# Graph attention, layer 3: the row of R of heads 1 to 3 by one bf16 matmul per block over an exact split in three parts

## The chip, the cores and the metric

The kernel runs on one core of one Trainium2 chip. The metric is the time of one execution on the device, in microseconds (us), lower is better. The engines are named as in the profile: PE (TensorE matmul), PEld (TensorE weight load), DVE (VectorE), ACT (ScalarE), POOL (GpSimd), SP (SyncE).

## The reference, cut to what matters

Sixteen graphs of 1024 nodes with 256 features pass four attention layers. In each layer the features are normalized, clipped at zero and projected, and every node takes a softmax-weighted mean over its neighbours. Layer 3 has four heads of 64 features each:

```python
h = einsum('bnd,hde->bhne', x, W)
e_src = einsum('bhne,hte->bhtn', h, a_src)
e_dst = einsum('bhne,hte->bhtn', h, a_dst)
weight = leaky_relu(e_src[:, :, 0, :, None] + e_dst[:, :, 0, None, :], 0.01)   # adj is 0 or 1: one type
attention = softmax(where(adj == 0, -1e9, weight), axis=-1)
dst = einsum('bhij,bhje->bhie', attention, h) + bias
out = relu(dst) + h          # then a layer norm over the 64 features of each head
```

The kernel doesn't form the logits. With s_i = e_src and d_j = e_dst, the exponential of leaky_relu(s_i + d_j) is the larger of exp(s_i + d_j) and exp(0.01 (s_i + d_j)). A factor exp(s_i) cancels in the softmax, and exp(0.01 d_j) is put into the values. What remains of a weight is max(C_j, R_i) where an edge is, and 0 elsewhere, with C_j = exp(0.99 d_j) and R_i = exp(-0.99 s_i). The change concerns how R gets to where it is used.

## The kernel before, in words

A short path (`short_path`) does the work; `general_path` is entered only if a flag says that the exponentials would be out of range. Each graph is a batch, worked by the generator `batch(b)`. Nodes are laid out as 8 blocks of 128: node blocks i are columns of a result, node blocks j are what is summed over and lie on the partitions.

For a layer, `weigh` makes the weights, transposed: 8 tiles of 128 nodes j by 1024 nodes i, in float32. It needs R_i as a row of 1024 elements that is the same on all 128 partitions. R is at hand as columns: for layer 3 in the tile `ex` (128 nodes x 8 blocks x 12 numbers: exp(0.01 d), C and R of the four heads). So `weigh` takes the PSUM tile `row` (two banks, one buffer for the whole kernel) and fills it by 8 transposes of PE (L314). Each has the column of one block, broadcast to 128 x 128, as its stationary operand and the identity as the moving one. Then DVE makes one weights tile per block j (L318), max(row, C_j) times the mask of edges. A list, `row_taken`, keeps two streams from holding the row at once.

In layers 0 to 2 (`attend`) PE multiplies the weights with the values V (L409, 128x128 tiles of the array). `project` turns the new features for the next layer (L290), ACT copies them (L292), PE projects them (L297), and ACT and DVE take them out of PSUM (L361, L365; in the projection for layer 3 L381, L382, with POOL writing V3 and adding beta, L384 to L389).

In layer 3 the loop over the heads h goes: the row and the weights of head 0 are started ahead of it; then for each head the row of head h + 1 is started, PE adds up the totals and values of head h in four 128x32 tiles of the array (L517), ACT copies the two accumulators (L579), PE turns them (L586, L594), and DVE, ACT and POOL scale and normalize (L487 to L502).

PSUM is full: `acc0` and `acc1` with two banks each, two buffers of `misc` (turned tiles of all kinds), and the row.

What sets the order: there are two streams, one of the even and one of the odd batches. Each generator yields estimated times, and the stream that is behind goes next (`streams`, with an offset `LAG`). So layer 3 of one batch is traced beside layers 0 to 2 of the next. The framework then lays each engine's queue at build time from this order and its own estimates of when inputs are ready; only instructions under `keep_in_program_order` are pinned. Each engine works its queue in order and waits on semaphores that the framework sets.

Of the kernel before, what the change touches and what calls it, by code (L numbers as in the profile page):

```python
# [32 lines left out]
F32 = mybir.dt.float32  # L33
BF = mybir.dt.bfloat16
# [7 lines left out]
P = 128  # L42
# [5 lines left out]
SLOPE = 0.2  # L48
L3_SLOPE = 0.01

REACH = 75.0


# [6 lines left out]
def short_path(ctx: ExitStack, tc: tile.TileContext, ins: dict, out: bass.AP, bad: bass.AP):  # L60

    nc = tc.nc
    x, adj = ins["x"], ins["adj"]
    B, N, D = x.shape
# [20 lines left out]
    make_identity(nc, ident)  # L85
    minus_half = const.tile([P, 1], F32, name="minus_half")
    nc.vector.memset(minus_half, -0.5)
    ones = const.tile([P, P], F32, name="ones")
    nc.vector.memset(ones, 1.0)

    squares = const.tile([P, B, NI], F32, name="squares")
    inverses = const.tile([P, B, NI], F32, name="inverses")
# [69 lines left out]
    def prepare():  # L162

        forms = [
            (SLOPE, 1 - SLOPE, SLOPE - 1),
            (-SLOPE, SLOPE - 1, 1 - SLOPE),
            (0.0, 1.0, -1.0),
            (L3_SLOPE, 1 - L3_SLOPE, L3_SLOPE - 1),  # L170
        ]
        scratch = [edges.tile([P, N], F32, name="weights1") for _ in EXT]

        def extend(l: int):
            n = EXT[l] // 3
            engine = nc.vector if l == 0 else nc.gpsimd
            for c, factor in enumerate(forms[l]):
                engine.tensor_scalar_mul(
                    W[l][:, :, D + c * n : D + (c + 1) * n],
                    wa[:, :, l : l + n, 0 if c == 2 else 1],  # L180
                    factor,
                )

        def fetch(l: int):
            def begin(dst: bass.AP, src: bass.AP):
                fetched = nc.sync.dma_start(dst, src)
                if l > 0:
                    tc.keep_in_program_order(fetched)

            if l < 3:  # L190
                begin(W[l][:, :, :D], ins[f"L{l}_W"].rearrange("(k p) o -> p k o", p=P))
                begin(scratch[l][:, : 2 * D], on_all_partitions(ins[f"L{l}_a"], 2 * D))
                return
            for k in range(NK):
                begin(
                    W[3][:, k, :D].rearrange("p (h e) -> p h e", h=H),
                    ins["L3_W"][:, ts(k, P), :].rearrange("h p e -> p h e"),
                )
            for s, name in enumerate(("L3_a_src", "L3_a_dst")):
                first = ins[name]  # L200
                begin(
                    scratch[3][:, ts(s, D)].rearrange("p (h e) -> p h e", h=H),
                    bass.AP(tensor=first.tensor, offset=first.offset, ap=[[0, P], [T * E, H], [1, E]]),
                )
            for t, a in ((bias, ins["L3_bias"]), (gamma, ins["L3_gamma"]), (beta, ins["L3_beta"])):
                begin(t, on_all_partitions(a, D))

        for l in range(3):
            fetch(l)
            yield  # L210
            for k in range(NK):
                for s in range(2):
                    prod = work.tile([P, D], F32, name="above", bufs=2)
                    made = nc.vector.tensor_tensor_reduce(
                        prod, W[l][:, k, :D], scratch[l][:, ts(s, D)], op0=ALU.mult, op1=ALU.add,
                        scale=1.0, scalar=0.0, accum_out=wa[:, k, l, s : s + 1],
                    )
                    if l > 0:
                        tc.keep_in_program_order(made)
            extend(l)  # L220
            yield
        fetch(3)
        yield
        for s in range(2):
            for k in range(NK):
                prod = work.tile([P, D], F32, name="above", bufs=2)
                tc.keep_in_program_order(
                    nc.vector.tensor_mul(prod, W[3][:, k, :D], scratch[3][:, ts(s, D)])
                )
                nc.vector.tensor_reduce(  # L230
                    wa[:, k, 3:, s], prod.rearrange("p (h e) -> p h e", h=H), AX.X, ALU.add
                )
        extend(3)

        tc.keep_in_program_order(nc.vector.tensor_scalar_add(beta, beta, -2.0))
        tc.keep_in_program_order(nc.vector.tensor_scalar_mul(gamma, gamma, ROOT_E))

        groups = (3 + H) * 2
        wa2 = small.tile([P, NK, groups], F32, name="wa2", bufs=1)
        nc.vector.tensor_mul(wa2, wa.rearrange("p k g s -> p k (g s)"), wa.rearrange("p k g s -> p k (g s)"))  # L240
        norms = psum.tile([P, 3 + H, 2], F32, name="misc")
        for k in range(NK):
            nc.tensor.matmul(
                norms.rearrange("p g s -> p (g s)"), ones, wa2[:, k],
                start=(k == 0), stop=(k == NK - 1),
            )
        both = small.tile([P, 3 + H], F32, name="both", bufs=1)
        nc.vector.tensor_reduce(both, norms, AX.X, ALU.add)
        worst = small.tile([P, 1], F32, name="worst", bufs=1)
        nc.vector.tensor_reduce(worst, both, AX.X, ALU.max)  # L250
        nc.vector.tensor_scalar(bad, worst, REACH * REACH / (2.0 * D), None, op0=ALU.is_gt)
        yield
# [50 lines left out]

    row_taken = []

    def weigh(b: int, column, c, op, into: list):


        while row_taken:
            yield 0.25  # L310
        row_taken.append(b)
        r = psum.tile([P, N], F32, name="row", bufs=1)
        for i in range(NI):
            nc.tensor.transpose(r[:, ts(i, P)], column(i).to_broadcast([P, P]), ident)  # L314
        yield 0.5
        for j in range(NI):
            w = edges.tile([P, N], F32, name=f"weights{b % 2}")
            nc.vector.scalar_tensor_tensor(w, r, c(j), masks[b][:, j // 2, :, j % 2], op0=op, op1=ALU.mult)  # L318
            into.append(w)
            if j == NI - 1:  # L320
                row_taken.pop()
            yield 0.5

    def start(behind, b: int):

        for t in behind:
            if row_taken == [b]:
                return
            yield t
# [19 lines left out]
    def batch(b: int):  # L349
# [43 lines left out]
        def attend(l: int, V: bass.AP, finish, then: int):  # L393

            weights = []
            behind = weigh(
                b, lambda i: V[:, i, D + 2 : D + 3], lambda j: V[:, j, D + 1 : D + 2],
                ALU.min if l == 1 else ALU.max, weights,
            )
            yield from start(behind, b)  # L400
            following = begin(then) if then < 3 else begin3()
            steps = iter(())
            accs = {}
            sums = small.tile([P, NI], F32, name="sums_of_x")

            def product(i: int, j: int):
                if j == 0:
                    accs[i] = accumulator(b)[:, : D + 1]
                nc.tensor.matmul(  # L409
                    accs[i], weights[j][:, ts(i, P)], V[:, j, : D + 1],  # L410
                    start=(j == 0), stop=(j == NI - 1),
                )


            for j in range(NI):
                next(behind)
                product(0, j)
                product(1, j)
                if b == 0 and j == NI - 1:


                    next(preparing)
                    if l == 0:
                        next(loading[1])
                    next(preparing, None)
                yield 0.9
            for _ in behind:
                pass
            for i in range(NI):
                if i > 1:  # L430
                    for j in range(NI):
                        product(i, j)
                acc = accs.pop(i)
                finish(i, acc, sums[:, i : i + 1])
                if i != 0:
                    yield 3.6
                if i % 2 == 1:

                    yield from steps
                    steps = project(b, then, xb, sums, i // 2, following[1])  # L440
                yield from islice(steps, 1)
            yield 1.0
            yield from steps
            return following[0]
# [61 lines left out]
        def weigh3(h: int):  # L506
            if h == H:
                return iter(())
            return weigh(
                b, lambda i: ex[:, i, 2 * H + h : 2 * H + h + 1],  # L510
                lambda j: ex[:, j, H + h : H + h + 1], ALU.max, weights,
            )

# [31 lines left out]

        behind = weigh3(0)
        yield from start(behind, b)
        for h in range(H):


# [461 lines left out]
```

## Time and profile before

| What | Value |
|---|---|
| Median of 3 runs | 3025.95 us (3025.94 to 3026.56) |
| Profiled execution | 3025.06 us, span 3023.3 us, granted PE clock 0.993 |
| Busy time: PE, PEld | 2905.2 us (96% of the span), 1960.1 us (65%) |
| Busy time: DVE, ACT, POOL | 2112.7 us (70%), 1092.1 us (36%), 964.5 us (32%) |
| Chain that ended last | PE 78%, DVE 12%, POOL 4%, ACT 4%, issue 2% |
| Rows of R of layer 3 (L314) | 512 PE instructions, 68.9 us busy, 276 ns each |
| Weights of layer 3 (L318) | 512 DVE instructions, 631.2 us busy, 1276 ns each |

Busy time is the time in which at least one instruction of the engine runs. PE's instructions overlap, so the busy time of a group is less than its count times its mean; the distance between two starts is what an instruction costs. The chain is followed back from the last instruction: at each step to what released it, or to the instruction before it on its engine.

### The profile page before, as it was taken

How to read it: one execution, taken by the hardware profiler on the slowest of the kernel's cores; microseconds unless marked ns; L12 is line 12 of the kernel's file. 1: busy time of each engine (PE TensorE's matmuls, PEld its weight loads, DVE VectorE, ACT ScalarE, POOL GpSimd, SP SyncE). 2: the span in 40 equal slices, each digit the busy share in tenths (PEclk: the TensorE clock that was granted, in tenths of full speed). 3: DMA queues.
4: the chain of work that ended last, by engine and by line, in shares of the span. 5: the costliest groups of instructions: out<-in, count | busy, mean ns of one | idle time of the engine just before them, and what ended most of it. 6: DMA issues, size and time to landing. Idle time of an engine off the chain costs nothing.

```text
span 3023.3 us, 44588 instructions
## 1 busy us (share of the span) xinstructions
PE 2905.2 (96%) x16774; PEld 1960.1 (65%) x16774; DVE 2112.7 (70%) x4467; ACT 1092.1 (36%) x3009; POOL 964.5 (32%) x1455
## 2 busy tenths in 40 slices
PE   7999999999999999999999999999999999999985
PEld 5775857658576675756758566585766857667551
DVE  5657687676866758677576875758667686675756
ACT  2333424243343433424334243433434334243331
POOL 2124324142232423324233242432324234242333
PEclk9999999999999999999999999999999999999997
DMA  7204023030321403122040220302204031110101
GB/s 122 37 8 63 29 29 56 8 49 29 36 49 14 71 2 49 36 28 57 5 50 31 29 56 8 50 29 32 53 11 56 19 50 36 15 29 5 19 21 30
DMA packets 120495, 106.11 MB, mean 35 GB/s; under 512 B 73680, under 2 KB 91216, under 8 KB 120272
## 3 DMA queue, kind: packets, MB, share of 16 engines
q0 software_dynamic: 40448, 67.12, 15.2%
q1 hardware_dynamic: 79824, 36.05, 5.9%
q8 instruction: 135, 2.21, 0.3%
q14 instruction: 88, 0.72, 0.1%
HBM read 153.49 MB, written 33.55 MB: 62 GB/s over the span
## 4 chain that ended last, share of the span: by engine, by line
PE 78%; DVE 12%; POOL 4%; ACT 4%; issue 2%; DMA 1%; SPq 0%; ACTq 0%; POOLq 0%; DVEq 0%
PE acc L409 39%; PE acc L517 21%; PE acc L297 11%; DVE weights L318 6%; PE misc L290 3%; PE row L314 2%; POOL rstd L261 2%; POOL y L487 1%; DVE y L500 1%; DVE V L365 1%; DVE var L496 1%; PE misc L594 1%; ACT adj_i L143 1%; ACT square L281 1%; PE misc L586 1%
## 5 line engine op out<-in xcount | busy, mean ns | idle before, releaser
L409 PE MATMUL acc<-V,weights 128*128 128x257 f32 x6144 | 1452.5, 386 | 24.6 <-ACT above L343 12.8
L409 PEld LDWEIGHTS acc<-V,weights 128*128 128x128 f32 x6144 | 1135.1, 190 | 338.3 <-DVE weights L318 92.7
L517 PE MATMUL acc<-weights,V 128*32 128x512 f32 x6144 | 756.4, 598 | 3.6 <-DVE weights L318 3.6
L318 DVE SCALAR_TENSOR_TENSOR weights<-row,ex,mask 128x1024 f32<-128x1024 f32 x512 | 631.2, 1276 | 91.0 <-PE acc L517 51.0
L297 PE MATMUL acc<-W,hT 128*128 128x259 f32 (+1 forms) x2048 | 522.1, 391 | 39.8 <-ACT hT L292 28.2
L297 PEld LDWEIGHTS acc<-W,hT 128*128 128x128 f32 x2048 | 376.5, 190 | 165.2 <-issue 49.5
L318 DVE SCALAR_TENSOR_TENSOR weights<-row,V,mask 128x1024 f32<-128x1024 f32 x384 | 475.4, 1276 | 7.7 <-PE row L314 7.7
L517 PEld LDWEIGHTS acc<-weights,V 128*32 128x32 f32 x6144 | 174.1, 109 | 379.6 <-issue 370.6
L341 ACT ACTIVATE below<-acc,inv 128x256 f32<-128x256 f32 x256 | 121.3, 474 | 681.0 <-DVE inv L334 404.1
L261 POOL TENSOR_TENSOR rstd<-rstd,minus_half 128x2 f32<-128x2 f32 (+1 forms) x320 | 307.7, 962 | 20.3
L281 ACT ACTIVATE square<-x_b,minus_mean 128x256 bf16<-128x256 f32 x512 | 259.2, 506 | 136.4 <-DVE minus_mean L271 131.7
L333 DVE TENSOR_SCALAR inv<-acc 128x1 f32<-128x1 f32 x256 | 39.7, 155 | 302.5 <-PE acc L409 299.0
L389 POOL TENSOR_TENSOR x_b<-x_b,beta 128x256 f32<-128x256 f32 x128 | 93.6, 731 | 491.1 <-ACT square L281 491.1
L579 ACT COPY sums<-acc 128x512 f32<-128x512 f32 x128 | 75.0, 586 | 413.9 <-PE acc L517 413.9
L260 POOL TENSOR_SCALAR rstd<-squared 128x2 f32<-128x2 f32 x256 | 59.5, 233 | 504.4 <-ACT square L281 503.6
L361 ACT ACTIVATE V<-acc,rstd 128x3 f32<-128x3 f32 x384 | 98.5, 262 | 315.2 <-PE acc L297 312.9
L292 ACT ACTIVATE hT<-misc 128x512 f32<-128x512 f32 x256 | 150.5, 594 | 155.4 <-PE misc L290 155.0
L365 DVE TENSOR_SCALAR V<-acc,rstd,V 128x256 f32<-128x256 f32 x256 | 133.1, 539 | 78.0 <-ACT V L361 77.2
L274 DVE TENSOR_SCALAR centered<-x_b,minus_mean 128x256 f32<-128x256 f32 x512 | 180.4, 383 | 4.3
L138 POOL DMA_DIRECT2D adj_i<-in_adj_dram x128 | 75.6, 590 | 331.0 <-ACT adj_i L143 262.2
L344 DVE SCALAR_TENSOR_TENSOR x_b<-below,x_b 128x256 f32<-128x256 f32 x256 | 117.7, 460 | 87.6 <-ACT below L341 87.4
L290 PE MATMUL misc<-ident,centered 128*128 128x128 f32 x1024 | 159.7, 278 | 15.7 <-DVE centered L274 13.8
(76 smaller groups left out, 2224.8 us busy)
## 6 DMA issues: line engine op xcount, KB each, us to landing
adj_i<-in_adj_dram POOLq DMA_DIRECT2D x128, 256.0 KB, 3.9
x_b<-in_x_dram SPq DMA_DIRECT2D x16, 1024.0 KB, 6.4
narrow<-in_adj_dram POOLq DMA_DIRECT2D x64, 256.0 KB, 9.5
out_dram<-y POOLq DMA_DIRECT2D x32, 512.0 KB, 7.5
mask<-narrow SPq DMA_TRANSPOSE x64, 4.3
W<-in_L_gnn_W_dram SPq DMA_DIRECT2D x3, 256.0 KB, 6.9
weights<-in_L_gnn_a_dram SPq DMA_DIRECT2D x3, 256.0 KB, 9.0
W<-in_L_gnn_W_dram SPq DMA_DIRECT2D x2, 128.0 KB, 7.9
```

What stands on the lines that cost most here:

```text
L261: nc.gpsimd.tensor_tensor(r, r, minus_half.to_broadcast([P, n]), op=ALU.pow)
L274: nc.vector.tensor_scalar(centered[:, n, :], xb[:, 2 * pair + n, :], minus_mean[:, n : n + 1], 0.0, op0=ALU.add, op1=ALU.max,)
L281: nc.scalar.activation(square, xb[:, 2 * pair + n, :], AF.Square, bias=minus_mean[:, n : n + 1], accum_out=squared[:, n : n + 1],)
L290: nc.tensor.transpose(turned[:, k, ts(n, P)], centered[:, n, ts(k, P)], ident)
L292: nc.scalar.mul(hT, turned, ROOT_D)
L297: nc.tensor.matmul(projected, hT[:, k, ts(n, P)], W[l][:, k, :], start=(k == 0), stop=(k == NK - 1),)
L318: nc.vector.scalar_tensor_tensor(w, r, c(j), masks[b][:, j // 2, :, j % 2], op0=op, op1=ALU.mult)
L341: nc.scalar.activation(below, acc[:, :D], AF.Exp, scale=inv)
L344: nc.vector.scalar_tensor_tensor(xi, below, 1.0, xi, op0=ALU.min, op1=ALU.add)
L365: nc.vector.tensor_scalar(V[:, i, :D], projected[:, :D], rstd, V[:, i, D : D + 1], op0=ALU.mult, op1=ALU.mult,)
L409: nc.tensor.matmul(accs[i], weights[j][:, ts(i, P)], V[:, j, : D + 1], start=(j == 0), stop=(j == NI - 1),)
L517: made = nc.tensor.matmul(accT[ts(n, QUAD), :], values, moving, start=first, stop=last)
```

## The change

R of heads 1 to 3 no longer goes through transposes of float32. After the row of head 0 has been started, POOL scales the 32 columns of R (8 blocks x 4 heads) by 65536 and splits them into three bf16 parts. Each part is what the ones before leave over, so that their sum is the float32 number. PE turns the three parts at once (128 x 96 to 96 x 128, in bf16, into a buffer of `misc`) and ACT copies the result to SBUF as `thirds_T`: partition 32 t + m holds part t of column m, where m = 4 i + h.

For a row, each block is then one bf16 matmul instead of a transpose. The stationary operand is column m of `rows_of` (96 x 32: three identities of 32 x 32 above each other, times 1/65536), broadcast to 96 x 128. The moving operand is `thirds_T`. It picks the three partitions of column m, adds them up in float32, and writes the sum to all 128 partitions. Head 0 keeps its transposes, as do the rows of layers 0 to 2. Set up once: `rows_of`, and `ident_bf`, a bf16 copy of the identity. The tile `ones` shrinks to one column, and its one user takes it broadcast.

```diff
@@ short_path, constants
-    ones = const.tile([P, P], F32, name="ones")
+    ones = const.tile([P, 1], F32, name="ones")
     nc.vector.memset(ones, 1.0)
+    rows_of = const.tile([3 * QUAD, QUAD], BF, name="rows_of")
+    for t in range(3):
+        nc.vector.tensor_scalar_mul(
+            rows_of[ts(t, QUAD), :], ident[ts(t, QUAD), ts(t, QUAD)], 1.0 / THIRDS
+        )
+    ident_bf = const.tile([P, P], BF, name="ident_bf")
+    nc.vector.tensor_copy(ident_bf, ident)
@@ prepare
-                norms.rearrange("p g s -> p (g s)"), ones, wa2[:, k],
+                norms.rearrange("p g s -> p (g s)"), ones.to_broadcast([P, P]), wa2[:, k],
@@ weigh
-    def weigh(b: int, column, c, op, into: list):
+    def weigh(b: int, turn, c, op, into: list):
...
-            nc.tensor.transpose(r[:, ts(i, P)], column(i).to_broadcast([P, P]), ident)
+            turn(r[:, ts(i, P)], i)
...
+    def along_row(column):
+        return lambda r, i: nc.tensor.transpose(r, column(i).to_broadcast([P, P]), ident)
@@ weigh3
+            def from_thirds(r: bass.AP, i: int):
+                m = i * H + h
+                row = rows_of[:, m : m + 1].to_broadcast([3 * QUAD, P])
+                nc.tensor.matmul(r, row, thirds_T, start=True, stop=True)
             return weigh(
-                b, lambda i: ex[:, i, 2 * H + h : 2 * H + h + 1],
+                b, from_thirds if h > 0 else along_row(lambda i: ex[:, i, 2 * H : 2 * H + 1]),
@@ batch, after the row of head 0 is started, ahead of the loop over the heads
         behind = weigh3(0)
         yield from start(behind, b)
+        rest = small.tile([P, NI, H], F32, name="rest", bufs=1)
+        nc.gpsimd.tensor_scalar_mul(rest, ex[:, :, 2 * H :], THIRDS)
+        thirds = small.tile([P, 3, NI, H], BF, name="thirds", bufs=1)
+        nc.gpsimd.tensor_copy(thirds[:, 0], rest)
+        nc.gpsimd.tensor_sub(rest, rest, thirds[:, 0])
+        nc.gpsimd.tensor_copy(thirds[:, 1], rest)
+        nc.gpsimd.tensor_sub(thirds[:, 2], rest, thirds[:, 1])
+        turned_thirds = psum.tile([3 * QUAD, P], BF, name="misc")
+        nc.tensor.transpose(turned_thirds, thirds.rearrange("p t i h -> p (t i h)"), ident_bf)
+        thirds_T = small.tile([3 * QUAD, P], BF, name="thirds_T", bufs=1)
+        nc.scalar.copy(thirds_T, turned_thirds)
         for h in range(H):
```

`THIRDS` is 65536.0, `QUAD` 32, `P` 128, `NI` 8, `H` 4.

More of the change, by code (lines that the diff above doesn't have):

```diff
@@ L49 @@
 L3_SLOPE = 0.01
+THIRDS = 65536.0
 REACH = 75.0
@@ L396, in attend @@
             behind = weigh(
-                b, lambda i: V[:, i, D + 2 : D + 3], lambda j: V[:, j, D + 1 : D + 2],
+                b, along_row(lambda i: V[:, i, D + 2 : D + 3]), lambda j: V[:, j, D + 1 : D + 2],
                 ALU.min if l == 1 else ALU.max, weights,
```

## The prediction

> **What bounds the kernel now.** I read the page's first part, then the stretches of the steady part, the groups by shape, the chain of waits, and the timelines of PE and POOL around one batch's layer 3.
>
> The page's first part, then one stretch of 184 us in the middle (busy us and instructions by engine, granted clock, DMA share, GB/s):
>
> ```profile
> PE 2905.2 (96%) x16774; PEld 1960.1 (65%) x16774; DVE 2112.7 (70%) x4467; ACT 1092.1 (36%) x3009; POOL 964.5 (32%) x1455
> ...
> 1420.00:1604.00 184.00, 180.61 (x1049) 121.98 (x1048) 131.11 (x277) 68.15 (x188) 60.42 (x91) 1.00 0.22 35
> ```
>
> The neighbouring stretch 1604 to 1788 has 180.61 us of PE again: the kernel repeats every 184 us, once per batch, and in each repetition PE idles 3.4 us. DVE is free for 53 us, ACT for 116, POOL for 124. So PE time taken out inside the steady part should come off the end nearly one for one, unless the instruction stands just ahead of one of the few places where PE waits anyway.
>
> The rows of R are this group (busy us, mean ns of one; then idle before):
>
> ```profile
> L314 PE MATMUL row<-ident,ex 128*128 128x128 f32 x512 | 68.9, 276 | 0.2 <-ACT ex L381 0.2
> ...
> L314 PEld LDWEIGHTS row<-ident,ex 128*128 128x128 f32 x512 | 56.9, 137 | 32.1 <-issue 13.4 <-DVE inv L333 10.9 <-DVE y L597 1.7
> ```
>
> 512 is 16 batches x 4 heads x 8 blocks. The 276 ns is a latency: the instructions overlap. Their spacing is what costs. In the timeline of PE:
>
> ```profile
> 1487.34 1.04 PE L314 MATMUL row<-ident,ex 128*128 128x128 f32 x8
> ...
> 1501.97 1.09 PE L314 MATMUL row<-ident,ex 128*128 128x128 f32 x8
> 1502.98 1.92 PE L517 MATMUL acc<-weights,V 128*32 128x512 f32 x16
> ...
> 1531.58 1.04 PE L314 MATMUL row<-ident,ex 128*128 128x128 f32 x8
> 1533.24 7.20 PE L409 MATMUL acc<-V,weights 128*128 128x257 f32 x32 [0.63 <-ACT above L343]
> ...
> 1546.67 1.09 PE L314 MATMUL row<-ident,ex 128*128 128x128 f32 x8
> ```
>
> These are heads 0, 1, 2 and 3 of one batch. (1.04 - 0.272)/7 = 0.110 us from one transpose to the next. In the chain of waits the same rows stand with 0.87 us after an L409 and 1.02 us after an L517:
>
> ```profile
> 1500.18 1.85 PE acc L517 x16
> 1502.04 1.02 PE row L314 x8
> 1503.05 1.85 PE acc L517 x16
> ```
>
> So a row costs 8 x 0.11 = 0.88 us, and 0.15 us more where it follows the 128x32 tiles. Heads 1 and 3 lie between instructions that wait for nothing: their time is on the path. Head 2 does not: behind it PE stands 0.63 us until ACT has freed an accumulator, and the chain goes back from there through ACT, DVE and POOL to the end of an L517 at 1525.7, not through the row. A shorter head-2 row only lengthens that stand.
>
> **What the Trainium skill says.** "TensorE: Matmul & The Clock Gate", section "Back-to-back issue gap": for bf16 N/2.4 + 2.5 ns alone, 56 ns at N=128, and about 81 ns for a sustained stream of weight load and matmul pairs. No bf16 matmul is in this trace; the 110 ns of the f32 transposes, about twice 56, [...]shows the 137 ns weight load hidden behind its neighbours. Same page, "Step-by-step: what each phase is for": PE pulls weight loads ahead, while matmuls stay in program order; so a PE instruction that waits holds all matmuls behind it. "TensorEngine Tiling (Array Packing)", "Key Properties": a change of tiling mode drains the array; the 1.02 against 0.87 us agrees, at 0.15 us.
>
> **The change part by part.** The sums are made against the profiled span, 3023.3 us (that execution took 3025.06; the runs 3025.94 to 3026.56), and the difference is then taken off the median 3025.95.
>
> *Rows of heads 1 to 3.* 24 f32 transposes of 0.110 us per batch become 24 bf16 matmuls of 128 columns, contraction over 96 partitions. Their spacing is not in the trace: 0.056 us is the lower bound, 0.110 us (a bf16 pair no faster than the f32 one) the upper, 0.081 the skill's sustained figure. I take 0.060, near the lower end, because the trace's weight loads are longer than the spacing and still hidden. A row falls from 0.88 to 0.48: 0.40 us off. The 0.15 us of the mode change stays. Heads 1 and 3: 2 x 0.40 = 0.80 us per batch on the path; head 2: nothing, for the reason above (upper bound its whole 0.40). For 15 batches: 12.0 us. The sixteenth runs alone at the end, where the chain goes through DVE's weights (L318) and POOL's y, so nothing is counted.
>
> *The turn of the thirds.* One bf16 transpose per batch on PE: bounded by 0.056 and by 0.11 plus a 0.15 us mode change; I take 0.10. 15 x 0.10 = 1.5 us lost.
>
> *Five POOL operations of 128x32.* The nearest rows are COPY 128x4 at 206 ns, TENSOR_SCALAR 128x8 at 275 and TENSOR_TENSOR 128x256 at 615; at 32 elements some 0.25 to 0.3 us each by interpolation, 1.3 to 1.5 us for the chain. POOL's timeline has room where they become ready:
>
> ```profile
> 1488.25 0.62 POOL L384 TENSOR_TENSOR V<-h,ex 128x256 f32<-128x256 f32 x1
> 1501.06 0.23 POOL L260 TENSOR_SCALAR rstd<-squared 128x2 f32<-128x2 f32 x1 [12.19 <-ACT square L281]
> ```
>
> The last ex is written at about 1487.8, POOL is done with V at 1488.9, and then has nothing for 12 us. The thirds would be ready at about 1490.4; the first row that needs them stands at 1502. Hidden: 0. Below zero is excluded, since nothing is taken off POOL; the upper bound is the first rival.
>
> *ACT's copy of 96x128.* Between the 0.27 us of a 128x12 ACTIVATE and the 0.59 us of a 128x512 COPY, say 0.3; ACT is idle from 1489.4 to 1499.4. Hidden: 0. It also holds one of the two misc buffers for about half a microsecond; the next user of misc after 1488.2 is at 1504.8. Buffers of one (rest, thirds, thirds_T) are reused a batch, 184 us, later: no wait.
>
> *Constants.* Four more DVE operations and a smaller memset at the start, under 1 us, while DVE waits for the first weights until 10.9 us. The norms' matmul with a broadcast operand runs once. 0.
>
> *Earlier weights of DVE.* A row that is 0.4 us shorter lets L318 begin sooner, where it waited for the row: 40.0 us over 64 rows in the group's idle time, most of it not at the heads that count (2.5 us in the whole stretch 1415 to 1604). PE is the bound, so 0, with a small gain possible.
>
> Sum: -12.0 + 1.5 = -10.5 us; 3025.95 - 10.5 = **3015.5**, 0.35% less. What a measurement of this kernel can tell from no change is about 0.2%, 6 us.
>
> **Rivals.**
>
> 1. *PE waits for the thirds (slower).* The turn is traced ahead of head 0's products, so it may stand in PE's queue right behind the row of head 0 and the L290 group, at 1488.65, while the thirds are ready at 1490.4. Then every matmul behind it waits: up to 1.8 us a batch, 27 us in all, less the 10.5 gained: +16.5, 3042.5. It decides from 0.7 us a batch (10.5/15), and the end is 0.2% slower from 1.1 us. For it: DVE waited for POOL's y (L487) 48 times, 30.5 us, so POOL arrives late where the queue's order counts on it. Against it: PE has a backlog at this place. Head 1's row went in 3.4 us after DVE let go of the buffer (the last L318 of head 0 ends at 1498.6), so the turn too probably finds other matmuls ahead of it.
>
> 2. *The weight load decides (no change).* At 0.081 us a row saves 0.23: 15 x (2 x 0.23 - 0.10) = 5.4 us, 3020.5; at 0.110 nothing is saved and 1.5 us lost, 3027.5. For it: the skill's sustained figure is measured, and weight loads of 128 columns take 137 ns here. Against it: they do not set the spacing in f32.
>
> 3. *Head 2 counts as well (faster by more).* If the stand behind head 2 moves or goes, its 0.40 us is gained too: 6 us more, 3009.5; with a spacing of 0.056 some 19 us in all (15 x (3 x 0.43 - 0.06) = 18.5), 3007.5. For it: the stand is 0.63 us of one order of the queues, and the added instructions can change that order. Against it: the chain behind it starts from PE 7.5 us earlier and runs through three engines.
>
> The order of the queues is laid by the framework's scheduler from its own costs. Five POOL instructions, one of PE and one of ACT more per batch and shorter rows can shift other work too, to either side; the trace cannot show it. It repeats in every batch, so 1 us a batch is 15 us: the range is stretched by it on both sides.
>
> **How the numbers follow.** The forecast (3007 to 3020) has 0.45, rival 3 and a luckier order 0.14, rival 2 0.18, rival 1 with an unluckier order 0.23. Faster by over 0.2% (below 3019.9): 0.45 + 0.14 = 0.59. Within 0.2%: 0.18. Slower: 0.23. The low end 3000 is rival 3 at its best with half a microsecond a batch from a new order; the high end 3042 is rival 1 at its full price. Beyond the two ends I leave 0.06 below and 0.12 above.
>
> **What would show it right or wrong.** The bf16 rows spaced about 0.06 us, so that eight take some 0.48 us plus the 0.15; the repetition 183.3 us instead of 184.0; PE's idle time per repetition about 3.8 us, the stand behind head 2 near 1.0. Rival 1 would show as PE idle before misc<-ident,thirds with POOL or DVE as releaser; rival 2 as rows of 0.65 us or more; a new order as other neighbours of the rows and other stands. The forecast is wrong if the rows shorten as said and the repetition does not.

## The result, and the profile after

The changed kernel takes 3046.41 us (median of 6 runs, 3044.95 to 3049.07), the kernel before 3025.77 us in the same comparison (6 runs, 3023.90 to 3026.56). The ratio is 1.007, with a 95% interval of 1.0057 to 1.0083: slower by 0.7%, 20.6 us, where 10.5 us less were forecast, and beyond the upper end of the range.

Lines of the changed kernel are numbered anew: L424 was L409, L539 was L517, L308 was L297, L301 was L290, L330 was L318. The f32 rows are L337, the bf16 rows L529, the turn of the thirds L579.

The page's first part, and one repetition of the steady part (busy us by engine as before):

```profile
PE 2897.3 (95%) x16790; PEld 1940.9 (64%) x16790; DVE 2104.1 (69%) x4471; ACT 1094.9 (36%) x3025; POOL 987.7 (32%) x1535
...
1420.00:1605.78 185.78, 180.49 (x1051) 120.86 (x1050) 130.59 (x277) 68.28 (x190) 61.89 (x96) 1.00 0.22 35
```

PE does less than before (2897.3 against 2905.2 us busy), and still the repetition is longer: 185.78 us instead of 184.03. PE idles 5.3 us in each, not 3.4. The groups by shape and the waits of PE say where (busy us, mean ns, then idle before; and: us in total, times, longest):

```profile
L529 PE MATMUL row<-thirds_T,rows_of 96*128 96x128 bf16 x384 | 29.7, 220 | 0.0
...
L579 PE MATMUL misc<-ident_bf,thirds 128*96 128x128 bf16 x16 | 4.1, 257 | 24.1 <-POOL thirds L577 24.1
```

```profile
PE misc L579 <- POOL thirds L577: 24.1, 16, 2.3
PE acc L424 <- ACT above L358: 19.3, 18, 1.6
```

The turn waits for POOL in every batch, 24.1 us in all. The second line was 12.8 us before: that is the stand (PE idle) behind head 2, grown as the row ahead of it shrank. The timeline of PE for the batch whose layer 3 lies where the one of the prediction lay:

```profile
1498.55 1.04 PE L337 MATMUL row<-ident,ex 128*128 128x128 f32 x8
1499.43 0.60 PE L424 MATMUL acc<-V,weights 128*128 128x257 f32 x2
1501.47 0.26 PE L579 MATMUL misc<-ident_bf,thirds 128*96 128x128 bf16 x1 [1.45 <-POOL thirds L577]
1501.57 0.61 PE L301 MATMUL misc<-ident,centered 128*128 128x128 f32 x4
...
1514.90 0.62 PE L529 MATMUL row<-thirds_T,rows_of 96*128 96x128 bf16 x8
1515.45 1.92 PE L539 MATMUL acc<-weights,V 128*32 128x512 f32 x16
...
1530.91 1.07 PE L539 MATMUL acc<-weights,V 128*32 128x512 f32 x8
1531.91 1.13 PE L424 MATMUL acc<-V,weights 128*128 128x257 f32 x4
...
1544.04 0.61 PE L529 MATMUL row<-thirds_T,rows_of 96*128 96x128 bf16 x8
1545.70 7.20 PE L424 MATMUL acc<-V,weights 128*128 128x257 f32 x32 [1.05 <-ACT above L358]
...
1577.23 1.04 PE L308 MATMUL acc<-W,hT 128*128 128x259 f32 x4
1578.20 1.04 PE L539 MATMUL acc<-weights,V 128*32 128x512 f32 x2
1579.18 1.14 PE L308 MATMUL acc<-W,hT 128*128 128x259 f32 x4
1580.25 5.35 PE L539 MATMUL acc<-weights,V 128*32 128x512 f32 x46
```

And the end of it in the kernel before:

```profile
1565.24 2.14 PE L297 MATMUL acc<-W,hT 128*128 128x259 f32 x8
1567.31 5.36 PE L517 MATMUL acc<-weights,V 128*32 128x512 f32 x48
1572.60 3.73 PE L409 MATMUL acc<-V,weights 128*128 128x257 f32 x16
```

Three things are to be seen.

- The turn stands behind a single product of 0.44 us and holds everything behind it for 1.45 us.
- A bf16 row takes 0.55 us to the next start, where an f32 row took 1.01. Behind head 2 it is 1.66 us to the next L424 in both kernels.
- At 1578.20 one matmul of head 3's sums (two records) has slipped between two pairs of projections; before, the eight records of L297 stood together and the 48 of L517 behind them. From start to start it takes 0.98 us, while in a full group of 16 records a matmul's share is 1.85/8 = 0.23. A group of eight records, one matmul in each of the four tiles, takes no longer than the lone one: 1.00 us (1530.91 to 1531.91). And the group that it has left saves nothing: its 46 records take 5.28 us to the next start at 1585.53, the 48 before took 5.29. So the 0.94 us in the last row of the table below is, by these figures, the time of one tile's work while the other three have none.

What POOL did meanwhile:

```profile
1499.44 0.32 POOL L572 TENSOR_SCALAR rest<-ex 128x32 f32<-128x32 f32 x1
1499.83 0.21 POOL L574 CAST thirds<-rest 128x32 bf16<-128x32 f32 x1
1500.12 0.25 POOL L575 TENSOR_TENSOR rest<-rest,thirds 128x32 f32<-128x32 f32 x1
1500.33 0.61 POOL L399 TENSOR_TENSOR V<-h,ex 128x256 f32<-128x256 f32 x1
1500.88 0.21 POOL L576 CAST thirds<-rest 128x32 bf16<-128x32 f32 x1
1501.17 0.25 POOL L577 TENSOR_TENSOR thirds<-rest,thirds 128x32 bf16<-128x32 f32 x1
```

The chain takes 2.0 us from its first start to its end, 0.55 of it from the start of a multiplication of V that stands in the middle to the next start. It begins at 1499.44, as the product ahead of the turn starts on PE.

Laid side by side, stretch by stretch from one row to the next, a repetition differs like this:

| Stretch of PE | Before | After | Difference |
|---|---|---|---|
| row of head 0 to row of head 1 (the turn) | 14.63 | 16.35 | +1.72 |
| row of head 1 to the row of V | 12.54 | 12.08 | -0.46 |
| row of V to head 2, and on to the L424 behind it | 18.73 | 18.72 | -0.01 |
| from there to head 3 | 13.43 | 13.43 | 0 |
| row of head 3 to the projections behind it | 2.86 | 2.40 | -0.46 |
| on to the projections at 1585.55 (1598.49 after) | 36.02 | 36.96 | +0.94 |

The sum is +1.73; the repetition grew by 1.75. DVE's first weights of the last batch's layer 3 start 24.5 us later (2955.84 against 2931.32 us). By the rows of head 0, the first repetition grew by only 0.77 us, since the kernel before has a lone matmul there too (at 277.04); the next 13 grew by 1.75 on average, and up to the last batch 1.08 were added. From there to the end it takes 88.7 us instead of 92.0, 3.3 less. 24.5 - 3.3 = 21.2, the difference of the two spans.

Not all of the 3.3 us is the rows'. In the last batch PE runs through most of head 0's sums in one group of 82 records, and in the kernel before it does so more slowly than in the kernel called rows alone below, behind an equal stand:

```profile
2933.94 11.30 PE L517 MATMUL acc<-weights,V 128*32 128x512 f32 x82 [2.66 <-DVE weights L318]
...
2932.34 9.60 PE L541 MATMUL acc<-weights,V 128*32 128x512 f32 x82 [2.66 <-DVE weights L332]
```

The first line is of the kernel before, with a granted clock of 0.91 in the first 20 us of this batch's layer 3; the second is of the rows alone, with 1.00. In the changed kernel the group takes 9.60 us too. So 1.7 of the 3.3 us go with the clock. The split alone, with f32 rows and a clock of 1.00 there, takes 90.3 us to the end; the rest, from 90.3 to 88.7, is the rows'. The end of a run can differ by some 3 us by the clock: with 0.83 in those 20 us the group took 12.45 and 12.52 us (row of head 2 alone; rows alone, pinned).

### The profile page after: what moved, and what is told of

Same layout as the page of the kernel before. It is cut to its first block, busy times and chain, and to the rows that moved or that the text cites. A ratio compares the mean times of both kernels' runs of the same rounds, so it can differ in the third digit from the quotient of the medians.

```text
span 3044.5 us, 44654 instructions
## 1 busy us (share of the span) xinstructions
PE 2897.3 (95%) x16790; PEld 1940.9 (64%) x16790; DVE 2104.1 (69%) x4471; ACT 1094.9 (36%) x3025; POOL 987.7 (32%) x1535
## 3 DMA queue, kind: packets, MB, share of 16 engines
q8 instruction: 135, 2.21, 0.3%
## 4 chain that ended last, share of the span: by engine, by line
PE 78%; DVE 11%; POOL 5%; ACT 4%; issue 1%; DMA 0%; ACTq 0%; SPq 0%; POOLq 0%; DVEq 0%
PE acc L424 39%; PE acc L539 23%; PE acc L308 10%; DVE weights L330 6%; PE misc L301 3%; POOL rstd L272 2%; PE row L337 1%; POOL y L502 1%; DVE y L515 1%; DVE V L380 1%; PE misc L628 1%; DVE var L511 1%; PE misc L620 1%; ACT square L292 1%; ACT adj_i L154 1%
## 5 line engine op out<-in xcount | busy, mean ns | idle before, releaser
L424 PE MATMUL acc<-V,weights 128*128 128x257 f32 x6144 | 1454.5, 386 | 31.6 <-ACT above L358 19.3
L424 PEld LDWEIGHTS acc<-V,weights 128*128 128x128 f32 x6144 | 1132.3, 190 | 344.7 <-DVE weights L330 94.7
L539 PE MATMUL acc<-weights,V 128*32 128x512 f32 x6144 | 769.0, 597 | 0.1
L330 DVE SCALAR_TENSOR_TENSOR weights<-row,ex,mask 128x1024 f32<-128x1024 f32 x512 | 633.1, 1277 | 81.9 <-PE acc L539 39.7
L308 PE MATMUL acc<-W,hT 128*128 128x259 f32 (+1 forms) x2048 | 522.0, 391 | 40.5 <-ACT hT L303 28.8
L308 PEld LDWEIGHTS acc<-W,hT 128*128 128x128 f32 x2048 | 376.2, 190 | 172.1 <-issue 49.5
L330 DVE SCALAR_TENSOR_TENSOR weights<-row,V,mask 128x1024 f32<-128x1024 f32 x384 | 475.4, 1276 | 8.2 <-PE row L337 8.2
L539 PEld LDWEIGHTS acc<-weights,V 128*32 128x32 f32 x6144 | 177.4, 109 | 374.2 <-issue 365.8
L301 PE MATMUL misc<-ident,centered 128*128 128x128 f32 x1024 | 159.5, 278 | 16.3 <-DVE centered L285 14.4
```

What stands on the lines that cost most here:

```text
L301: nc.tensor.transpose(turned[:, k, ts(n, P)], centered[:, n, ts(k, P)], ident)
L308: nc.tensor.matmul(projected, hT[:, k, ts(n, P)], W[l][:, k, :], start=(k == 0), stop=(k == NK - 1),)
L424: nc.tensor.matmul(accs[i], weights[j][:, ts(i, P)], V[:, j, : D + 1], start=(j == 0), stop=(j == NI - 1),)
L539: made = nc.tensor.matmul(accT[ts(n, QUAD), :], values, moving, start=first, stop=last)
```

## The experiments

The theory was: PE, the bound, waits at the turn for POOL; the lone matmul takes away what the shorter rows give. Rival A: the wait is only displaced, and PE would stand elsewhere without it. Rival B: the bf16 rows, mixed among f32 work, are what costs. The repetition in the table is the distance from one appearance of the same piece of DVE's weights in the chain of waits to the next; it varies by some hundredths of a microsecond, except in the longer chain. Each ratio is against runs of the kernel before in the same comparison, whose medians were 3024.29 to 3025.77 us. The last column is said of the steady part; the kernel before and the split alone have such a matmul once, in the first batch.

| Kernel | Median us | Ratio to before (95%) | Repetition us | Wait at the turn | Lone matmul |
|---|---|---|---|---|---|
| before | 3025.77 | | 184.03 | | no |
| after | 3046.41 | 1.007 (1.0057 to 1.0083) | 185.78 | 1.45 | yes |
| turn later | 3021.83 | 0.999 (0.9981 to 0.9999) | 184.09 | 0 | yes |
| turn without its wait | 3024.03 | 0.9997 (0.9988 to 1.0006) | 184.17 | 0 | yes |
| split alone | 3048.49 | 1.0076 (1.0059 to 1.0093) | 185.72 | 1.44 | no |
| rows alone | 3020.54 | 0.9987 (0.998 to 0.9994) | 184.04 | | yes |
| row of head 2 alone | 3035.25 | 1.0033 (1.0021 to 1.0046) | 184.97 | | yes |
| rows alone, pinned | 3008.64 | 0.9945 (0.9928 to 0.9962) | 183.24 | | no |
| pin alone | 3034.50 | 1.0033 (1.0021 to 1.0046) | 184.95 | 1.44 | no |
| turn later, pinned | 3010.43 | 0.9953 (0.9936 to 0.9969) | 183.31 | 0 | no |
| longer chain | 3080.11 | 1.018 (1.0163 to 1.0197) | 186.7 or 188.25 | 2.31 | yes |

**The turn later.** The turn and ACT's copy move into the loop over head 0's products (the lines that go are not shown):

```diff
                     add_values(h, j)
+                    if j == 2:
+                        turned_thirds = psum.tile([3 * QUAD, P], BF, name="misc")
+                        turn = nc.tensor.transpose(
+                            turned_thirds, thirds.rearrange("p t i h -> p (t i h)"), ident_bf
+                        )
+                        tc.keep_in_program_order(turn)
+                        thirds_T = small.tile([3 * QUAD, P], BF, name="thirds_T", bufs=1)
+                        nc.scalar.copy(thirds_T, turned_thirds)
                     yield 1.8
```

> The turn of the thirds and its copy are traced after the first half of head 0's products (j = 2) and pinned there on PE; everything else is as in the changed kernel. Theory (PE waits for POOL at the turn, 1.60 us a batch from start to start, 24 us in 15 batches): the wait goes and the time falls from 3046.4 to about 3022. Rival A (the wait is only displaced: PE would stand a little later for DVE's first weights tiles or for ACT anyway): 3038 to 3046, with a new stand on PE near the old place. Rival B (the rows or the mixing of bf16 and f32 cost it): 3044 or more.

Measured 3021.83 us. In PE's timeline of this kernel the turn now comes without a wait and is followed at once, 8.8 us after the row of head 0:

```profile
1488.14 1.04 PE L337 MATMUL row<-ident,ex 128*128 128x128 f32 x8
...
1496.92 0.26 PE L591 MATMUL misc<-ident_bf,thirds 128*96 128x128 bf16 x1
1497.01 0.66 PE L308 MATMUL acc<-W,hT 128*128 128x259 f32 x2
```

The next instruction of PE, an L308, starts 0.09 us later. No other stand takes its place: the repetition loses 1.69 us. Rival A falls. Rival B falls as the cause of the 1.69 us, since all the bf16 rows are still there.

**The turn without its wait.** The turn stays early, but reads something that is always ready (R of heads 1 to 3 is then not the reference's):

```diff
-        nc.tensor.transpose(turned_thirds, thirds.rearrange("p t i h -> p (t i h)"), ident_bf)
+        nc.tensor.transpose(turned_thirds, ident_bf[:, : 3 * QUAD], ident_bf)
```

> The turn takes the bf16 identity in place of the thirds, so that R of heads 1 to 3 is not the reference's; POOL's five operations, the turn, ACT's copy and the rows all stay. Theory (the wait for POOL): about 3022, as with the turn traced later. Rival A (displaced): 3038 to 3046. If POOL's operations cost by themselves (delaying V or other work of POOL), both this and the later turn stay above 3030.

Measured 3024.03 us, with POOL's five operations still running. Here the turn stands right behind the row of head 0, and PE doesn't wait at it. The operations cost next to nothing by themselves: with them, the turn and the copy, the repetition is 184.09 (turn later) and 184.17 us, and 184.04 without any of them (rows alone, below).

**The split alone.** All rows as before; split, turn and copy stay, and nobody reads the result:

```diff
-                b, from_thirds if h > 0 else along_row(lambda i: ex[:, i, 2 * H : 2 * H + 1]),
+                b, along_row(lambda i: ex[:, i, 2 * H + h : 2 * H + h + 1]),
```

> The split, the turn and the copy stay, and nobody reads the result: the rows of all heads are f32 transposes again. In the queue of PE the turn stands as in the changed kernel, and the lone L517 matmul between two pairs of projections is gone. Theory: before plus wait and turn, 15 x (1.60 + 0.10) = 25.5 us: about 3051. Rival B (the rows cost it): 3026 to 3030.

Measured 3048.49 us, 1.69 us a repetition more than before: nearly all of the 1.75, with no bf16 row and no lone matmul in the steady part.

```profile
1502.61 0.26 PE L579 MATMUL misc<-ident_bf,thirds 128*96 128x128 bf16 x1 [1.44 <-POOL thirds L577]
```

**The rows alone.** No split, turn or copy (the lines that go are not shown); the rows read a constant (R of heads 1 to 3 is not the reference's):

```diff
+    thirds_T = const.tile([3 * QUAD, P], BF, name="fixed_T")
+    nc.vector.memset(thirds_T, 1.0)
```

> No split, no turn, no copy: the bf16 rows of heads 1 to 3 read a constant set once, so that R of heads 1 to 3 is not the reference's. In the queue of PE the lone L517 matmul between two pairs of projections is there. Theory (rows save 2 x 0.46 us a batch on the path, the lone matmul costs 0.94): -13.8 + 14.1 us and some 3 us off in the last batch: about 3022 to 3026. If the lone matmul costs nothing by itself: about 3009. Rival B (the rows cost it): above 3030.

Measured 3020.54 us, a little below what was expected. The repetition is 184.04 us, as before the change: what two rows save, 0.92 us, and what the lone matmul takes, 0.94, cancel. The 5 us that are left come from outside the steady part, 3.4 of them in the last batch (88.6 us to the end instead of 92.0), of which 1.7 go with the granted clock, as said above.

**The row of head 2 alone.**

```diff
-                b, from_thirds if h > 0 else along_row(lambda i: ex[:, i, 2 * H : 2 * H + 1]),
+                b, from_thirds if h == 2 else along_row(lambda i: ex[:, i, 2 * H + h : 2 * H + h + 1]),
```

This is made on the rows alone (R of head 2 is not the reference's).

> Only the row of head 2 in bf16, from a constant (R of head 2 is not the reference's), without the split; heads 1 and 3 as before. The queue of PE has the lone L517 matmul again. Theory (head 2's saving is lost in the stand behind it, the lone matmul costs 0.94 us a batch): 14 us slower than before, about 3039. If head 2's saving counts after all: 3033 or less. If the lone matmul costs nothing: 3025.

Measured 3035.25 us, some 4 us below what was expected; the execution that was profiled took 3038.07, with the slower end told of above. The repetition is longer by 0.94 us, the price of the lone matmul to the hundredth, and the row of head 2, 0.43 us shorter, gives nothing back. A shorter instruction makes the kernel 0.3% slower, because it changes the order of the queue. In its timeline of PE:

```profile
1536.68 0.61 PE L531 MATMUL row<-fixed_T,rows_of 96*128 96x128 bf16 x8
1538.34 7.20 PE L426 MATMUL acc<-V,weights 128*128 128x257 f32 x32 [1.05 <-ACT above L360]
...
1571.31 1.05 PE L541 MATMUL acc<-weights,V 128*32 128x512 f32 x2
```

**Pinning the lone matmul.** The first matmul of head 3's sums is held behind what is traced ahead of it on PE. A matmul is pinned when the list `pinned` isn't empty, so that otherwise the first of a group goes free:

```diff
-                pinned = []
+                pinned = [None] if h == 3 and first == 0 else []
```

With the rows alone:

> The bf16 rows alone, from a constant (R of heads 1 to 3 is not the reference's), with the same pin. Theory: 14 us less than the rows alone: about 3006; what is left against before is the rows' own saving, 2 x 0.46 us a batch and some us in the last batch. Rival: as the rows alone, 3020.

Measured 3008.64 us. With the turn later:

> The turn traced later, and the first L517 matmul of head 3 pinned behind what is traced ahead of it on PE, so that the lone L517 matmul no longer stands between two pairs of projections; in its place stands one transpose of a row of V. Theory (a lone matmul in one 128x32 tile, with two changes of tiling mode, costs 0.94 us a batch): 14 us less than the turn traced later alone, about 3008. Rival (the lone matmul lies where PE would stand anyway, and the period is set elsewhere): 3019 to 3022.

Measured 3010.43 us, the best of the kernels that compute all of the reference. In the hole between the two pairs of projections now stands one transpose of a row of V, in the same tiling mode, for 0.26 us from start to start:

```profile
1558.28 1.04 PE L308 MATMUL acc<-W,hT 128*128 128x259 f32 x4
1559.16 0.27 PE L337 MATMUL row<-ident,V 128*128 128x128 f32 x1
1559.42 1.15 PE L308 MATMUL acc<-W,hT 128*128 128x259 f32 x4
```

The pin gives 0.78 us a repetition here and 0.80 with the rows alone, not all of the 0.94: with the transpose between them the two pairs take 2.21 us (1558.28 to 1560.49), against 3.02 with the lone matmul and 2.07 before. With the changed kernel:

> The changed kernel with the pin alone: the lone L517 matmul goes, the turn stays where PE waits for it. Theory (wait and lone matmul add up, each by itself): 0.78 us a repetition less than the changed kernel, as the pin gave with the turn traced later, so 185.0 us, and 12 us less in all: about 3034. If the two are not independent: 3040 or more, or below 3028.

Measured 3034.50 us and 184.95 us a repetition, 0.83 less than the changed kernel: wait and lone matmul add up.

**The longer chain.** The last of POOL's operations is made five times over:

```diff
         nc.gpsimd.tensor_sub(thirds[:, 2], rest, thirds[:, 1])
+        for _ in range(4):
+            nc.gpsimd.tensor_sub(thirds[:, 2], rest, thirds[:, 1])
```

> The changed kernel with the last of POOL's five operations made five times over (four more of some 0.25 us, each waiting for nothing but its place): the dose of the wait. The turn stands one product of layer 0 to 2 (0.43 us) later in PE's queue, the rest of the queue is the same. Theory (PE waits for the end of POOL's chain): 4 x 0.25 to 0.31 less 0.43, so 0.6 to 0.8 us a batch more, 9 to 12 us: 3055 to 3058. If the wait is set by something else than the chain's length: 3046 or less.

Measured 3080.11 us, some three times the added loss that was expected. The wait grew as the theory has it, by 0.86 us, to 2.31, and the repetitions that show only this take 186.7 us, 0.9 more than the changed kernel's. But most take 188.25: two repetitions of this kind and one of the other, in turn. The stretches of one of the long ones (columns as before: PE, PEld, DVE, ACT, POOL, granted clock) show why:

```profile
1513.00:1517.20 4.20, 1.94 (x13) 1.45 (x11) 3.09 (x3) 0.66 (x3) 3.48 (x12) 1.00 0.00 0
1517.20:1519.20 2.00, 1.95 (x9) 1.67 (x10) 2.00 (x3) 0.86 (x2) 0.00 (x0) 0.63 0.04 8
1519.20:1521.20 2.00, 2.00 (x8) 0.82 (x10) 0.96 (x1) 0.00 (x0) 0.00 (x0) 0.52 0.00 0
1521.20:1523.20 2.00, 2.00 (x18) 0.73 (x11) 0.00 (x0) 0.00 (x0) 0.00 (x0) 1.00 0.00 0
```

Behind the stand PE's granted clock is 0.63 and 0.52 for 4 us. In the changed kernel it stays at 1.00 behind the stand of 1.45 us. The dose is confirmed by the repetitions without this, and a second cost has come on top. What makes the clock fall behind two stands out of three of the same length was not tried.

## Why the prediction was wrong, point by point

- **The bound**, PE, and "nearly one for one": right: about 1.60 us of wait and 0.10 of turn came out as 1.69 us of repetition (split alone).
- **The rows**: right. Spacing taken 0.060 us, measured (0.62 - 0.220)/7 = 0.057; a row 0.46 us cheaper, taken 0.40. The 81 ns that the Trainium skill ("TensorE: Matmul & The Clock Gate", "Back-to-back issue gap") has for a sustained stream of pairs do not hold here. So the rival "the weight load decides" falls.
- **Head 2 gives nothing**: right, 1.66 us before and after, and shown by the row of head 2 alone. The rival "head 2 counts as well" falls.
- **The turn itself**, 0.10 us: right (1501.47 to 1501.57).
- **The last batch**, taken as 0: it gave 3.3 us, about half of it by the granted clock, which is luck, and half by the shorter rows (90.3 to 88.7), which the sum left out.
- **"Five POOL operations ... Hidden: 0": the step that failed.** I set the chain's end, about 1490.4, against the first row that reads the result, at 1502, and found 12 us of room. But the first to wait for POOL is not the row; it is the turn, and a matmul that waits holds all matmuls behind it, as I had quoted from "Step-by-step: what each phase is for" of the same page. The trace agrees: 24.1 us of PE's waits lie at the turn. The chain's end was not the fault: taken 3.06 us behind the start of head 0's row (1490.4 less 1487.34), measured 2.87 (1501.42 less 1498.55).
- **The rival "PE waits for the thirds"** named the mechanism, the place and the price: up to 1.8 us a batch, measured 1.45 idle and about 1.6 from start to start. What I held against it, a backlog of PE at this place, was wrong: the scheduler put the turn behind 0.44 us of work. Why so early was not tried on its own. The longer chain gives a hint: for four more operations, 1.22 us on POOL, the scheduler moved the turn by one product, 0.43 us. That its price for POOL's operations is too low would fit, but is not shown.
- **The order of the queues** was said to be able to cost 1 us a batch. It cost 0.94, by one matmul of the 128x32 tiles standing alone. I treated this and the rival as alternatives: 3042 holds one of them. Both came: -0.92 + 1.72 + 0.94 = +1.74 a repetition. The sum itself put the order of the queues at nothing. The kernel before has one such matmul, at 277.04 in its first batch, where the two pairs take 3.03 us instead of 2.07: its price could have been read there, though not that the change would repeat it in every batch.

## What to carry to other kernels

When work is split over engines, look for the first instruction in the bound engine's queue that waits for the new chain, not for the last user of its result; if that instruction is early, trace it later and pin it there. When a scheduler orders the queues, even an instruction that only gets shorter can move another one: compare the order before and after, and look above all for a matmul of a tiled group that has been left alone. The same change with the turn placed later and one pin takes 3010.43 us, a ratio to before of 0.9953 (0.9936 to 0.9969), against 1.007 as it stands. Its repetition of 183.31 us is the 183.3 that the prediction named as a sign of being right, in part by luck: the rows save 0.12 us more than was taken, and the two pairs of projections take 0.14 more than before, which was not foreseen.

## What the runs showed of the hardware that was not expected

One f32 matmul of 512 columns in a single 128x32 tile, between matmuls of the full array, takes 0.98 us of PE from start to start, and four of them, one in each tile, take 1.00; in a longer group over the four tiles each one's share is 0.23.

A stand of PE of 2.3 to 2.7 us can be followed by a lower granted clock. Behind the stand of 2.31 us of the longer chain it fell in 11 of the first 15 batches (0.63 and 0.52 over two stretches of 2 us in the one shown), and the repetition was 1.55 us longer (188.25 against 186.7); in the other 4 it stayed at 1.00. Behind the stand of 2.66 us in the last batch it fell in the kernel before and not in the rows alone. A stand of 1.45 us never did this: in the changed kernel the next L539 starts 2.36 or 2.37 us behind the turn in all of the first 15 batches. "TensorE: Matmul & The Clock Gate", section "Part 1: The HAM clock gate (the "warmup" mystery)", puts the return to half clock behind an idle window of about 3.4 us; here less than that was enough. The length of the stand alone does not decide it, and where the limit lies was not tried.
